# A graph layer with 1,327 row gathers: each gather from the table also waits for the landing of the gather three in front of it

## The chip, the cores and the metric

The kernel runs on one core of a Trainium2 chip. The time is device microseconds (us) of one execution of the program. The kernel before was timed three times: 2152.66, 2145.68 and 2149.95 us, a median of 2149.95 us. The profile comes from a further execution of its own, with a time of 2145.14 us, whose instructions span 2143.3 us.

The engines are named as in the profile: PE (matmul), PEld (PE's weight load), DVE (vector), ACT (scalar), POOL (GpSimd), SP (sync). Here POOL issues the gathers, SP and ACT issue the other DMAs.

## The reference: what is computed

```python
x, src, dst, edge                     # (12500, 64), (200000,), (200000,) sorted, (200000, 32)
msg_in     = concat([x[src], x[dst], edge])                 # 200000 x 160
messages   = relu(msg_in @ mW1 + mb1) @ mW2 + mb2           # hidden 128, out 64
aggregated = segment_sum(messages, dst, 12500)
update     = relu(concat([x, aggregated]) @ uW1 + ub1) @ uW2 + ub2
out        = layernorm(x + update)
```

The edges are sorted by their destination, so the destinations of neighbouring edges lie in a short window of nodes. The sources are random, so `x[src]` needs a real gather.

## The kernel before

The 200,000 edges are cut into 1,563 tiles of 128 edges, and six tiles make a step (`SUB = 6`), 261 steps in all. In a setup phase PE multiplies all nodes by the source part of `mW1` and by the destination part (`products`, L637), and the results go to tables in DRAM: `tab_a` by ACT's queue (L649), `tab_b` with the bias by SP's (L658). A row of a table is 128 floats, 512 bytes. From then on each step does this:

- **Gather** (`fetch`, L237). For a tile of the step, one indirect DMA issued by POOL fetches 128 rows of `tab_a`, those of the tile's 128 sources, into the step's buffer `xg`, 64 KB. In the first eight steps (`XG = 8`) the table is not ready yet, and 48 gathers fetch rows of `x` instead, which PE transposes and multiplies (L324, L427). In 118 steps (`COPIED`) two of the six tiles aren't gathered: ACT and DVE copy the nodes one column at a time from a transposed `x` that lies on chip (L379, L387), and PE multiplies them (L411). So 1,279 gathers read `tab_a`.
- **Edge part** (`edge_part`, L408). SP loads the edge features and the destinations into `l`, and windows of `tab_b` into `rhs`; DVE turns destinations into a selection (L271, L279). PE multiplies `l` by `rhs` into `pc`.
- **Node part** (`node_part`, L435). PE adds the gathered rows to `pc` by a matmul with the identity, four matmul records a step. This is the only reader of a gather from `tab_a`.
- **Sum** (`positive`, `collect`). DVE applies relu (L448), and one step later PE adds the result into the destinations' sums (L481) and counts (L477). Every few steps a block of nodes is finished (`update`, `residual`, `norm`, `store`).

The order is written out by hand in one loop over the steps. In the loop, `gather(s)` takes a buffer and lists the gathers of a step, `frees` says which earlier step must have been read for that, and `gathered <= s + XG` keeps gathers up to eight steps ahead of the step in which PE reads them; there are nine buffers (`ROWB = 9`). `fetch` issues one gather. Its argument `behind` names an instruction of PE (or, in the setup, of ACT) whose end the gather waits for, so that the gathers of a step are spread over it:

```python
for u in units[:1] if paced else units:
    fetch(u)
...
done = collect(s - 1)
n = (len(units) + 1) // 2
for k in range(n):
    fetch(units.pop(0), done[(k + 1) * len(done) // n - 1])
```

POOL's queue holds nothing but gathers from the setup to the end of the loop. Each gather reports its landing on one of eight semaphores in turn (`DMASW0` to `DMASW7`), and a gather waits until the one eight in front of it, the last user of its semaphore, has landed.

Of the kernel before, what the change touches and what calls it, by code (L numbers as in the profile page):

```python
# [37 lines left out]
XG = 8  # L38
# [34 lines left out]
U8 = mybir.dt.uint8  # L73
YBASE = XBASE + 4 * XCOLS
LEAD = 8
PACE = ((11, 0.48), (50, 0.505), (130, 0.483), (170, 0.469), (261, 0))
FINAL = 258


def progress(s):  # L80

    return sum(r * max(0, min(s + 1, b) - a) for (a, r), (b, _) in zip(PACE, PACE[1:]))

# [42 lines left out]
def gnn_kernel(ctx: ExitStack, tc: tile.TileContext, x1T, x, eT, e_rows, src, src_row, dst, dst_row, wlist, wrow, wnext, whalf,  # L126
# [77 lines left out]
    wb = const.tile([SUP, NSUP], I32, name="wb")  # L204

    rows = ctx.enter_context(tc.tile_pool(name="rows", bufs=ROWB))
    xg = {}

    def frees(s):

# [22 lines left out]
    def fetch(unit, behind=None):  # L233

        s, i = unit
        t, a = s * SUB + i, xg[s][1]
        ins = nc.gpsimd.indirect_dma_start(  # L237
            out=a[:, i, :] if s < XG else a[:, i // 2, i % 2, :], out_offset=None, in_=A[:, :] if s >= XG else x[:, :],
            in_offset=bass.IndirectOffsetOnAxis(ap=src_s[:, t:t + 1], axis=0))
        if behind is not None:  # L240
            tc.add_manual_dep(ins.ins, behind.ins.name,
                              mybir.DependencyInfo(mybir.DependencyClass.Sync, mybir.DependencyReason.DATA), reason="pace")

    with tc.tile_pool(name="work", bufs=2) as work, tc.manual_schedule():
# [83 lines left out]
        def columns_list():  # L328

            cols = work.tile([P, 2, 2, P], I32, name="cols", tag="tb", bufs=4)  # L330
            for r in range(2):
                n = min(P, NSUB - 1 - LEAD - r * P)
                v = src_row[:, ((LEAD + r * P) * SUB + SUB - 2) * P:]
                nc.sync.dma_start(cols[:n, r].rearrange("k b e -> k (b e)"),
# [6 lines left out]
        def portion(s, own):  # L341

            found = []
            for j, c in enumerate(COPIED):
                total = own(j)
                lo, hi = (min(max(int((progress(s + d) - j) * total / CHUNK + 1e-6) * CHUNK, 0), total) for d in (-1, 0))
                if lo < hi:
                    if c not in xc:
                        xc[c] = work.tile([P, P], F32, name="xc", bufs=3)
                    found.append((xc[c], c - LEAD, lo, hi, j))  # L350
            return found
# [347 lines left out]
        for u in first[:AHEAD]:  # L699
            fetch(u)  # L700
# [18 lines left out]
        for k, c in enumerate(range(0, NB, NCH)):  # L719
            copied = chunk_a(c)  # L720
            for i, u in enumerate(first[:EACH]):
                fetch(u, None if i else copied)
            first = first[EACH:]
            if k == 2:
                chunk_b(0, [B0v, Bv])
            if k == 3:
                nc.vector.tensor_tensor(drc[:, :8 * SUP], dst_s[:, :8 * SUP], early, op=ALU.subtract)
                first_nodes(0, 8)
            if k == 4:

                w0 = wint[:, :GE * SUP // SUB * LS]
                nc.vector.tensor_scalar(past, w0[:, GE * SUP // SUB * LS - 1:], float(EARLY - WIN), None, op0=ALU.is_gt)
                nc.vector.tensor_scalar(w0, w0, float(EARLY - WIN), None, op0=ALU.min)
                windows(0)
                windows(1)
            if k in (5, 7):
                g = (k - 5) // 2
                select_rows(g)
                load(g)
                select(g)  # L740
                counts(g)
            if k == 10:
                offsets()
# [97 lines left out]
        for s in range(last + 2):  # L841
# [6 lines left out]
            for u in units[:1] if paced else units:  # L848
                fetch(u)
# [267 lines left out]
```

## Time and profile before

| what | number |
|---|---|
| runs | 2152.66, 2145.68, 2149.95 us; median 2149.95 us |
| profiled execution: time, span | 2145.14 us, 2143.3 us |
| busy: PE, ACT, POOL, DVE | 1701.7, 1573.7, 1253.8, 1132.0 us |
| mean granted TensorE clock | 0.782 of full speed |
| DMA moved, mean rate | 190.59 MB, 89 GB/s |
| gathers from `tab_a`: number, issued from, to | 1,279, 80.3 us, 2091.3 us |
| the matmuls that read them: first, last start | 141.9 us, 2123.6 us |

In the lines of the profile, `L237 POOL DMA_INDIRECT xg<-tab_a,src_s x1279` is a group of instructions: source line, engine, operation, what is written and read, and how many. "busy" is the time for which such an instruction ran on its engine; for a gather that is the making of its descriptors, and the bytes move later. "idle before" is the engine's idle time ahead of the group with what ended it: "issue" means nothing that the profile shows, "remote" a semaphore whose writer the profile doesn't have. The chain is the work that ended last, followed back from the end of the program; a piece "DMA xg<-tab_a,src_s" in it runs from the issue of a gather to the semaphore of its landing. q0 is the queue of the gathers, q1 that of SP's DMAs, q10 that of ACT's.

### The profile page before, as it was taken

How to read it: one execution, taken by the hardware profiler on the slowest of the kernel's cores; microseconds unless marked ns; L12 is line 12 of the kernel's file. 1: busy time of each engine (PE TensorE's matmuls, PEld its weight loads, DVE VectorE, ACT ScalarE, POOL GpSimd, SP SyncE). 2: the span in 40 equal slices, each digit the busy share in tenths (PEclk: the TensorE clock that was granted, in tenths of full speed). 3: DMA queues.
4: the chain of work that ended last, by engine and by line, in shares of the span. 5: the costliest groups of instructions: out<-in, count | busy, mean ns of one | idle time of the engine just before them, and what ended most of it. 6: DMA issues, size and time to landing. Idle time of an engine off the chain costs nothing.

```text
span 2143.3 us, 50649 instructions
## 1 busy us (share of the span) xinstructions
PE 1701.7 (79%) x10742; PEld 1279.7 (60%) x10742; DVE 1132.0 (53%) x8036; ACT 1573.7 (73%) x8029; POOL 1253.8 (59%) x1336
## 2 busy tenths in 40 slices
PE   3487778797787788877888878887878888888788
PEld 3365556565565566656566656665665666666566
DVE  2215655565555555565555545455555565555553
ACT  1155887669869797798687877787867877787872
POOL 6565665666666656555655555565556656556660
PEclk7667887877787877777787877788778878887889
DMA  8452333332222223232233323233333333333331
GB/s 231 125 130 75 96 87 96 89 92 71 80 74 78 77 76 80 76 85 78 76 82 83 88 78 88 80 94 84 82 89 81 86 93 88 88 88 87 85 92 51
DMA packets 207847, 190.59 MB, mean 89 GB/s; under 512 B 57909, under 2 KB 174093, under 8 KB 207549
## 3 DMA queue, kind: packets, MB, share of 16 engines
q0 software_dynamic: 42464, 85.48, 16.1%
q1 hardware_dynamic: 150396, 92.86, 15.4%
q10 hardware_dynamic: 14690, 8.99, 1.5%
q8 instruction: 101, 1.65, 0.3%
q14 instruction: 196, 1.61, 0.2%
HBM read 169.15 MB, written 18.02 MB: 87 GB/s over the span
## 4 chain that ended last, share of the span: by engine, by line
PE 64%; issue 18%; DVE 9%; another core or an unknown queue 3%; DMA 2%; POOL 2%; DVEq 1%; ACT 0%; SPq 0%; ACTq 0%; POOLq 0%
PE sums L481 20%; PE pc L435 17%; PE pc L408 13%; DVE xc L387 4%; PE cnt L477 3%; DVE h L448 2%; PE cps L545 2%; PE cps L543 2%; POOL xg L237 2%; PE pc L411 2%; PE sums L529 2%; PE sums L530 1%; DVE l L271 1%; DMA xg<-tab_a,src_s 1%
## 5 line engine op out<-in xcount | busy, mean ns | idle before, releaser
L237 POOL DMA_INDIRECT xg<-tab_a,src_s x1279 | 1207.3, 944 | 812.5 <-issue 263.1
L379 ACT ACTIVATE xc<-xtop,xbot 128x1 f32 x7872 | 1490.7, 280 | 183.6 <-issue 161.6
L387 DVE TENSOR_TENSOR xc<-xtop,xbot 128x1 int32 x7232 | 607.2, 155 | 472.0 <-issue 457.8
L481 PE MATMUL sums<-band,h 128*128 128x96 f32 x3126 | 532.7, 324 | 134.8 <-issue 86.3
L481 PEld LDWEIGHTS sums<-band,h 128*128 128x128 f32 x3126 | 470.0, 230 | 170.0 <-issue 106.3
L435 PE MATMUL pc<-xg,band 128*128 128x384 f32 (+1 forms) x1008 | 465.4, 590 | 34.8 <-issue 30.7
L408 PE MATMUL pc<-rhs,l 64*128 64x128 f32 x3126 | 371.7, 354 | 77.2 <-issue 60.8
L408 PEld LDWEIGHTS pc<-rhs,l 64*128 64x128 f32 x3126 | 294.5, 238 | 123.9 <-issue 90.9
L448 DVE TENSOR_SCALAR h<-pc 128x768 f32<-128x768 f32 x252 | 240.3, 953 | 202.4 <-PE sums L481 83.7
L435 PEld LDWEIGHTS pc<-xg,band 128*128 128x128 f32 x1008 | 223.2, 244 | 154.8 <-issue 106.9
L271 DVE TENSOR_TENSOR l<-l,cps 128x768 f32<-128x768 int32 (+1 forms) x134 | 127.1, 949 | 146.1 <-PE pc L435 41.0
L477 PEld LDWEIGHTS <-one 128*1 128x1 bf16 x1563 | 59.5, 81 | 225.0 <-issue 218.9
L477 PE MATMUL cnt<-band,one 128*1 128x32 bf16 x1563 | 100.8, 180 | 54.6 <-issue 53.5
L552 ACT ACTIVATE y<-cps 128x256 f32<-128x256 f32 (+1 forms) x36 | 13.6, 379 | 157.5 <-issue 91.9
L411 PE MATMUL pc<-band,xc 64*128 64x128 f32 x472 | 80.4, 318 | 23.0 <-issue 19.3
L535 ACT ACTIVATE hTu<-sums,ub_s 128x416 f32<-128x416 f32 (+1 forms) x36 | 21.6, 599 | 100.9 <-remote 35.5
L279 DVE TENSOR_TENSOR band<-cps,drc 128x384 f32<-128x384 f32 x131 | 71.6, 546 | 25.4 <-PE pc L408 24.5
L637 PE MATMUL pb<-band,xtop 64*128 64x128 f32 x200 | 45.9, 395 | 42.8 <-DVE tb L645 21.9
L411 PEld LDWEIGHTS pc<-band,xc 64*128 64x128 f32 x472 | 64.2, 229 | 22.8 <-issue 22.5
L637 PEld LDWEIGHTS pb<-band,xtop 64*128 64x128 f32 x200 | 39.0, 283 | 47.6 <-DVE tb L645 23.0
L237 POOL DMA_INDIRECT xg<-in_x,src_s x48 | 45.5, 948 | 25.3 <-issue 13.5
L545 PE MATMUL cps<-u2c,hTu 128*128 128x64 f32 x284 | 54.4, 342 | 6.4 <-issue 6.0
(104 smaller groups left out, 630.5 us busy)
## 6 DMA issues: line engine op xcount, KB each, us to landing
l<-in_dst_row SPq DMA_DIRECT2D x262, 96.0 KB
l<-in_eT SPq DMA_DIRECT2D x262, 96.0 KB
xg<-tab_a,src_s POOLq DMA_INDIRECT x1279
rhs<-tab_b SPq DMA_DIRECT2D x361, 32.0 KB
tab_b<-tb SPq DMA_DIRECT2D x13, 512.0 KB
rhs<-tab_b SPq DMA_DIRECT2D x387, 16.0 KB
tab_a<-tb ACTq DMA_DIRECT2D x12, 512.0 KB
out<-y SPq DMA_DIRECT2D x35, 128.0 KB
```

The source lines that it names most:

```text
L237: ins = nc.gpsimd.indirect_dma_start(out=a[:, i, :] if s < XG else a[:, i // 2, i % 2, :], out_offset=None, in_=A[:, :] if s >= XG else x[ ...
L271: nc.vector.tensor_tensor(l[r], l[r].bitcast(I32), node[r].unsqueeze(2).broadcast_to([r.stop - r.start, SUP // 2, P]), op=ALU.is_equal)
L379: nc.scalar.activation(o[:, e:e + 1], top.bitcast(F32), AF.Identity, bias=bot.bitcast(F32))
L387: nc.vector.tensor_tensor(o[:, e:e + 1].bitcast(I32), top.bitcast(I32), bot.bitcast(I32), op=ALU.bitwise_or)
L408: done = nc.tensor.matmul(pc[:, b, k, :], L[g][q:q + 64, m, :], rhs[g % 2][q:q + 64, w, :], start=k == 0, stop=False)
L411: done = nc.tensor.matmul(pc[:, b, k, :], xc[s][q:q + 64], w1a[q:q + 64], start=False, stop=False)
L435: added = nc.tensor.matmul(pc[:, b, :m], ident, a[:, b, :m], start=False, stop=True)
L448: nc.vector.tensor_scalar(h, pc, 0.0, None, op0=ALU.max)
L477: nc.tensor.matmul(pn[:, bass.ds(ws[i], WIN)], one, SB[g][:, k0 + i, :, 1], start=False, stop=ends and i == n - 1)
L481: made.append(nc.tensor.matmul(ps[:, bass.ds(ws[i], WIDE * WIN)], h[:, i % 2, i // 2, :], widened(g, k0 + i), start=False, stop=ends and i ...
L545: nc.tensor.matmul(py[:, i], hT[:, i * P:(i + 1) * P], u2c, start=False, stop=i + 1 == blocks(u))
L637: nc.tensor.matmul(pb[:, h, i, :], (xbot if h else xtop)[64 * h:64 * h + 64, (c + HB * h + i) * P:(c + HB * h + i + 1) * P], w[64 * h:64 * ...
```

## The change

A list keeps every gather that was issued. A gather that reads `tab_a` gets a second dependency: besides the instruction `behind`, it waits for the semaphore of the gather three in front of it (`flight[-3:][:1]`). The gathers of the first eight steps get none.

```diff
+FLIGHT = 3
...
-    xg = {}
+    xg, flight = {}, []
...
         ins = nc.gpsimd.indirect_dma_start(
             out=a[:, i, :] if s < XG else a[:, i // 2, i % 2, :], out_offset=None, in_=A[:, :] if s >= XG else x[:, :],
             in_offset=bass.IndirectOffsetOnAxis(ap=src_s[:, t:t + 1], axis=0))
-        if behind is not None:
-            tc.add_manual_dep(ins.ins, behind.ins.name,
+        waited = [] if s < XG or len(flight) < FLIGHT else flight[-FLIGHT:][:1]
+        flight.append(ins)
+        for other in waited + [behind] * (behind is not None):
+            tc.add_manual_dep(ins.ins, other.ins.name,
                               mybir.DependencyInfo(mybir.DependencyClass.Sync, mybir.DependencyReason.DATA), reason="pace")
```

No instruction changes its place on any engine, and no wait changes on PE, DVE, ACT or SP. Only the waits of POOL's gathers differ. The first gathers from `tab_a` on POOL, before; `DMAHW` are semaphores of the setup's stores to the table, `DMASW` those of gathers:

```order
L237 DMA xg_452<-tab_a_63,src_s_68 128x128 [waits DMAHW4_49,DMAHW3_49,DMAHW5_49,DMAHW2_49,DMAHW7_49,DMAHW0_49,DMASW0_49]
L237 DMA xg_452<-tab_a_63,src_s_68 128x128 [waits DMASW1_49]
L237 DMA xg_452<-tab_a_63,src_s_68 128x128 [waits DMASW2_49]
L237 DMA xg_452<-tab_a_63,src_s_68 128x128 [waits DMASW3_49]
L237 DMA xg_452<-tab_a_63,src_s_68 128x128 [waits DMASW4_49]
```

The same five gathers after:

```order
L238 DMA xg_452<-tab_a_63,src_s_68 128x128 [waits DMAHW3_49,DMAHW4_49,DMAHW2_49,DMAHW5_49,DMAHW0_49,DMAHW7_49,DMASW5_49,DMASW0_49]
L238 DMA xg_452<-tab_a_63,src_s_68 128x128 [waits DMASW6_49,DMASW1_49]
L238 DMA xg_452<-tab_a_63,src_s_68 128x128 [waits DMASW7_49,DMASW2_49]
L238 DMA xg_452<-tab_a_63,src_s_68 128x128 [waits DMASW3_49,DMASW0_49]
L238 DMA xg_452<-tab_a_63,src_s_68 128x128 [waits DMASW4_49,DMASW1_49]
```

These five wait for one semaphore more each, until the wait for the third in front implies that for the eighth.

In the loop, on POOL at a place some thirty steps in, before; `PE` is the pacing instruction:

```order
L237 DMA xg_7324<-tab_a_63,src_s_68 128x128 [waits DMASW4_49]
L237 DMA xg_7324<-tab_a_63,src_s_68 128x128 [waits DMASW5_49,PE_49]
L237 DMA xg_7324<-tab_a_63,src_s_68 128x128 [waits DMASW6_49,PE_49]
L237 DMA xg_7324<-tab_a_63,src_s_68 128x128 [waits DMASW7_49,PE_49]
L237 DMA xg_7699<-tab_a_63,src_s_68 128x128 [waits DMASW0_49]
```

The same gathers after:

```order
L238 DMA xg_7324<-tab_a_63,src_s_68 128x128 [waits DMASW1_49]
L238 DMA xg_7324<-tab_a_63,src_s_68 128x128 [waits DMASW2_49,PE_49]
L238 DMA xg_7324<-tab_a_63,src_s_68 128x128 [waits DMASW3_49,PE_49]
L238 DMA xg_7324<-tab_a_63,src_s_68 128x128 [waits DMASW4_49,PE_49]
L238 DMA xg_7699<-tab_a_63,src_s_68 128x128 [waits DMASW5_49]
```

Each gather has as many waits as before. The wait for the semaphore of the eighth in front (its own number) has turned into one for that of the third in front, five numbers further.

## The prediction

> **What bounds the kernel now.** I read the page first: how busy the engines are, what the chain that ended last consists of, and what the gathers look like in the groups.
>
> ```profile
> span 2143.3 us, 50649 instructions
> PE 1701.7 (79%) x10742; PEld 1279.7 (60%) x10742; DVE 1132.0 (53%) x8036; ACT 1573.7 (73%) x8029; POOL 1253.8 (59%) x1336
> ...
> PE 64%; issue 18%; DVE 9%; another core or an unknown queue 3%; DMA 2%; POOL 2%; DVEq 1%; ACT 0%; SPq 0%; ACTq 0%; POOLq 0%
> ...
> L237 POOL DMA_INDIRECT xg<-tab_a,src_s x1279 | 1207.3, 944 | 812.5 <-issue 263.1
> ```
>
> PE is the bound: 79% busy and 64% of the chain, while POOL is 59% busy and 2% of the chain. POOL has 812.5 us of idle time in front of its gathers, so it can be held up by much in sum before it runs short. The question is where a single wait would fall, and whether PE would notice.
>
> For that I read the lines of the gather and of the matmul that reads it (the view by source line), for their first and last starts.
>
> ```profile
> L237 POOL DMA_INDIRECT xg<-tab_a,src_s x1279: 938/944/1475, 80.3 to 2091.3; - x183
> L237 POOLq EVENT_SEMAPHORE  x1034: 17/17/43, 12.4 to 2087.0; - x173
> ...
> who waited for it (us, times):
>   PEld pc L435: 5.1, 9
>   PE pc L408: 4.5, 4
> ```
> ```profile
> L435 PE MATMUL pc<-xg,band x1008: 376/486/1009, 141.9 to 2123.6; 128*128 128x384 f32 x87, 128*128 128x256 f32 x81
> ```
>
> The first gather is issued at 80.3 and its reader starts at 141.9: 61.6 us ahead. At the end it is 2091.3 against 2123.6, still 32.3 us. In between the code holds eight steps of lead, and a step lasts (2123.6 − 141.9) / 252 = 7.9 us (1,008 reading matmuls, four a step), so a step's gathers are begun some 60 us before they are read. The few microseconds that "who waited for it" puts on gathers (the largest 5.1 us in 9 times) can hardly be that: the matmul waits on several semaphores, each shared by every eighth gather, and a gather for a later step that lands in that moment moves the same semaphore. I take them as put down wrongly, and price the other reading among the rivals.
>
> Next, how close together gathers come, on POOL's timeline at the place where DMA is fullest:
>
> ```profile
> 102.07 0.94 POOL L237 DMA_INDIRECT xg<-tab_a,src_s  x1 [0.30 <-issue]
> 103.32 0.94 POOL L237 DMA_INDIRECT xg<-tab_a,src_s  x1 [0.30 <-issue]
> 104.57 0.94 POOL L237 DMA_INDIRECT xg<-tab_a,src_s  x1 [0.30 <-issue]
> 105.82 0.95 POOL L237 DMA_INDIRECT xg<-tab_a,src_s  x1 [0.30 <-issue]
> 108.69 0.94 POOL L237 DMA_INDIRECT xg<-tab_a,src_s  x1 [1.93 <-PE pc L408]
> 109.94 0.94 POOL L237 DMA_INDIRECT xg<-tab_a,src_s  x1 [0.30 <-issue]
> ```
>
> Even unhindered, a gather starts 1.25 us after the last one (0.94 of work and 0.30 of pause). So the third in front was started at least 105.82 − 102.07 = 3.75 us earlier. **The new wait costs nothing where a gather lands, and POOL takes note, within 3.75 us.** How long a landing takes stands in the chain, in nine pieces spread over the program; here are the first, the shortest, the two longest and the last:
>
> ```profile
> 400.26 2.31 DMA xg<-tab_a,src_s
> 652.90 3.35 DMA xg<-tab_a,src_s
> ...
> 1255.47 2.23 DMA xg<-tab_a,src_s
> ...
> 1726.21 3.48 DMA xg<-tab_a,src_s
> ...
> 2028.39 2.29 DMA xg<-tab_a,src_s
> ```
>
> They run from 2.23 to 3.48 us, mostly near 2.3. What POOL needs after a semaphore wait is passed stands in the chain between 393 and 394 us: 0.02 for the wait, then 0.21 to the start of the gather.
>
> ```profile
> 393.46 0.02 POOLq L237
> 393.47 0.21 issue
> 393.68 0.94 POOL xg L237
> ```
>
> **The change part by part.**
>
> *The wait in the loop.* 2.31 + 0.23 = 2.54 us against 3.75: 1.2 us to spare. The longest, 3.48 + 0.23 = 3.71, still fits by 0.04. In flight before the change are therefore, at the moment a gather is issued, two others as a rule; the new limit is already kept. Cost 0 for nearly all of the 1,279. A gather that lands later than 3.5 us would delay the next but two by the excess, a few tenths. What is queued behind the waiting gather is only more gathers, since nothing else is in POOL's queue there; and who waits for those is PE's L435, tens of microseconds later. The cover is that lead, 32 us at its shortest. If it were gone, every tenth would count once, on the step that reads the gather.
>
> *The wait in crowded stretches.* The setup's transfers and the first steps' large loads overlap the first gathers. By stretches:
>
> ```profile
> 80.00:100.00 20.00, 11.38 (x105) 9.24 (x104) 2.78 (x4) 2.53 (x5) 13.20 (x14) 0.83 0.53 137
> 100.00:112.00 12.00, 7.69 (x67) 6.45 (x68) 1.26 (x3) 4.58 (x6) 7.94 (x9) 0.80 0.78 188
> 120.00:130.00 10.00, 8.04 (x48) 6.71 (x48) 0.95 (x1) 4.67 (x5) 6.49 (x7) 0.67 0.84 187
> 140.00:150.00 10.00, 9.20 (x53) 5.80 (x51) 1.82 (x2) 7.69 (x6) 6.27 (x8) 0.77 0.70 157
> 1200.00:1600.00 400.00, 326.18 (x2005) 241.61 (x2004) 217.59 (x1598) 309.84 (x1608) 236.04 (x251) 0.79 0.31 84
> ```
>
> The last but one number is the DMA engines' busy share: 0.53 to 0.84 in four stretches up to 150 us, 0.31 in the middle of the program. In the second of them, DMA by queue from 99.5 us to 108.4, and to 108.6:
>
> ```profile
> q1 hardware_dynamic: 1015, 1.34, 65.9%
> q0 software_dynamic: 95, 0.20, 13.2%
> ...
> xg<-tab_a,src_s POOLq DMA_INDIRECT x6
> ```
> ```profile
> q0 software_dynamic: 96, 0.20, 12.9%
> ```
>
> Over the program q0 moved 42,464 packets for 1,327 gathers, 32 each:
>
> ```profile
> q0 software_dynamic: 42464, 85.48, 16.1%
> ```
>
> Six gathers were issued from 99.5 on, and by 108.4 only 95 packets had moved: the third of them, that of 102.07, was one packet short of its end and finished by 108.6, some 6.4 us after its issue. The gather of 105.82 would now wait for it and start near 108.5 + 0.23 = 108.7, 2.9 us late. The one of 108.69 then can't start before 108.7 + 1.25 = 110.0, 1.3 us late, and the lateness goes at the next pause that PE sets (such as the 1.93 us in front of 108.69). So four stretches with about 3 us of lateness at most in each, on a dozen gathers whose readers start at 141.9 us and after, with up to 61.6 us of lead: cost 0.
>
> *The bounds of that.* From above: if each of the four delays reached PE in full, 4 × 2.9 = 11.6 us. From below: a gather that is held back leaves the DMA engines to SP's loads, and something does wait for these:
>
> ```profile
> DVE drc L592 <- DMA col_a<-in_wrow: 14.4, 2, 10.7
> ```
>
> A gather's part of the DMA engines there is 13.2% of 8.9 us for 95 packets, so 0.4 us for 32. Up to two gathers are held back in each stretch: 4 × 2 × 0.4 = 3.2 us of gain at most, if all of it lay on the chain. I take 0, nearest to the rows of the lead and of the loads (13.2% against 65.9% of the DMA, so the loads are late by themselves), and keep −3.2 and +11.6.
>
> *Added instructions.* The first five gathers from the table wait for one semaphore more each, at 17 ns a wait: 0.09 us, in POOL's idle time. Cost 0. PE, DVE, ACT and SP have the same instructions and waits.
>
> *A rule weighed.* The longest of all 1,279 gather issues took 1.475 us, the median 0.944; even the longest would add 0.53 us to the landing, 2.84 + 0.23 = 3.07 of 3.75. The Trainium skill, in "SBUF — State Buffer", section "A bandwidth-pool intuition that's wrong", says that a DMA issued from GpSimd which takes some 620 ns alone takes some 3,100 ns beside a vector copy in a two-port mode, because GpSimd can't write descriptors meanwhile. By that, an estimate from the page: a landing of 2.31 + 2.48 = 4.8 us, a gather each (4.8 + 0.23) / 3 = 1.68 us, 2,145 us in all instead of 2,011, and a time of some 2,280 us. This trace shows no such gather before the change.
>
> *The sum.* 2145.14 us for the profiled execution, plus 0. That execution lies 4.8 us below the median of the three runs, so the forecast for the median is 2149.9 us. Runs of this kernel lie within 0.3% of each other (2145.68 to 2152.66), and a change below 0.3%, 6.4 us, can't be told from none.
>
> **The rivals.**
>
> 1. *Slower: the late gathers reach PE.* Place: the steps after 141.9 us. For it speak the 5.1 us in 9 times in which PE is said to have waited for gathers; against it the 61.6 us of lead there. It decides from the point where lateness is handed from stretch to stretch until it exceeds the lead, or where the lead of a single gather is below 3 us. Price 11.6 us: 2161.5 us.
> 2. *Slower: landings are longer for POOL than the pieces show,* so that the limit of three sets the rate. POOL has (2091.3 − 80.3) / 1279 = 1.57 us for a gather, so three in flight suffice up to a landing of 3 × 1.57 − 0.23 = 4.5 us. Against it: the longest of nine pieces is 3.48. If all landed as in the crowded stretch, after 6.4 us, a gather would take (6.4 + 0.23) / 3 = 2.21 us and all of them 2,827 instead of 2,011: some 2,960 us; with landings of 4.6 us it would be some 40 us. The rule of the Trainium skill's page "SBUF — State Buffer" that was weighed above is one way into this rival.
> 3. *Faster: fewer gathers among the loads.* Speaking for it: DVE's 14.4 us behind one of the loads. Price 3.2 us at most, 2146.7, which is inside what can't be told; for 6.4 us sixteen gathers would have to move out of the way of loads that the chain waits for.
> 4. *The limit never binds at all,* not even in the crowded stretches, because spacing by PE is wider than there. Then the time is the same 2149.9, and only the trace could tell.
>
> **How the numbers follow.** The forecast and rival 4, no change within 0.3%: 81%. Rival 1: 6%; rival 2, mostly in a weak form: 3%; slower for a reason that I don't see, 3%: 12% slower. Rival 3 or an unseen gain beyond 0.3%: 7%. The range takes the runs' own spread (−4.3, +2.7) and the two bounds: 2149.9 − 4.3 − 3.2 = 2142 below, and 2149.9 + 11.6 = 2162 above.
>
> **What would show it.** In the profile of the changed kernel: gathers still 1.25 us apart within a step from 200 us on, POOL's idle sum near 812 us, and the first and last reader at 142 and some 20 us before the end as now. Between 80 and 155 us a gather of four or so per stretch should start up to 3 us later, with a landing of a gather named as what ended POOL's wait. Wrong would be: POOL waiting for DMA all through the program, PE's L435 waiting for gathers by more than a few microseconds in sum, or SP's loads before 150 us ending clearly earlier.

## The result and the profile after

The changed kernel takes 2170.2 us (median, 2164.64 to 2173.93), the kernel before beside it 2148.07 us: a ratio of 1.0093, 95% interval 1.0073 to 1.0113. It is slower by some 20 us (22 by the medians, 20 by the ratio). The forecast was no change, with a range up to 2162.

The lines of the page that answer to those shown of before, then those of the gather and of its reader by source line (the change moves L237 to L238 and L435 to L438), and POOL's waits by what ended them:

```profile
span 2172.1 us, 50654 instructions
PE 1698.7 (78%) x10742; PEld 1282.5 (59%) x10742; DVE 1132.1 (52%) x8036; ACT 1576.5 (73%) x8029; POOL 1253.6 (58%) x1336
...
L238 POOL DMA_INDIRECT xg<-tab_a,src_s x1279 | 1207.1, 944 | 839.0 <-issue 258.2
```
```profile
L238 POOL DMA_INDIRECT xg<-tab_a,src_s x1279: 938/944/1140, 87.5 to 2115.4; - x183
...
L438 PE MATMUL pc<-xg,band x1008: 376/486/1009, 130.0 to 2149.2; 128*128 128x384 f32 x87, 128*128 128x256 f32 x81
```
```profile
POOL xg L238 <- DMA xg<-tab_a,src_s: 57.9, 75, 4.9
```

No engine does more work, and the new wait holds POOL for 57.9 us in 75 places, 4.9 us at the longest. The first reader starts at 130.0 us, 11.9 us *earlier* than before; the last one 25.6 us later. So it is not a delay that adds up from the start. Where the time goes is read from the readers: for each step, the start of its first L438 in the trace, minus the start in the trace of before.

```
step         8      9     10     11     12     13     14     20     32     64    128    192    256
after    -11.9  -11.7  -18.3  -18.8  -10.6   17.7   14.9   21.6   16.2   18.0   20.3   21.8   25.6
```

Up to step 11 the kernel is ahead by up to 18.8 us. Between the readers of steps 11 and 13 it loses 36 us, and after that next to nothing: 8 us over 243 steps. The same stretch in windows, after and then before (the columns are the window, its length, busy time of PE, PEld, DVE, ACT and POOL with their instructions, the granted clock, the DMA engines' share, GB/s):

```profile
100.00:120.00 20.00, 17.76 (x191) 15.49 (x190) 4.54 (x7) 13.01 (x13) 9.41 (x10) 0.93 0.68 166
120.00:140.00 20.00, 17.53 (x116) 13.26 (x116) 3.00 (x4) 17.06 (x13) 7.96 (x10) 0.66 0.80 178
140.00:160.00 20.00, 13.74 (x81) 8.33 (x82) 6.83 (x34) 0.00 (x0) 13.75 (x15) 0.85 0.29 77
160.00:200.00 40.00, 10.95 (x38) 6.92 (x39) 3.08 (x15) 0.00 (x0) 25.80 (x28) 0.50 0.20 51
```
```profile
100.00:120.00 20.00, 13.73 (x109) 11.59 (x109) 2.44 (x5) 7.99 (x10) 12.85 (x14) 0.68 0.59 144
120.00:140.00 20.00, 16.55 (x104) 14.13 (x106) 1.51 (x2) 9.59 (x9) 12.99 (x14) 0.67 0.59 133
140.00:160.00 20.00, 16.37 (x83) 11.35 (x82) 3.61 (x6) 12.87 (x9) 12.63 (x15) 0.67 0.55 132
160.00:200.00 40.00, 25.71 (x155) 17.82 (x153) 19.03 (x99) 16.46 (x89) 23.44 (x25) 0.71 0.30 80
```

From 100 to 140 us POOL issues 20 gathers instead of 28, and PE runs 307 matmuls instead of 213. From 160 to 200 us PE runs 38 instead of 155, while DMA is at 0.20. The early gain shows in PE's waits from 80 to 145 us; these are all that end by issue, first before, then after:

```profile
PE pc L427 <- issue: 13.6, 5, 7.8
PE pc L408 <- issue: 4.0, 7, 1.3
```
```profile
PE pc L411 <- issue: 2.2, 3, 1.1
PE cnt L480 <- issue: 0.5, 1, 0.5
```

What POOL does there and what PE does there stand on their timelines in the kernel after:

```profile
111.78 0.94 POOL L238 DMA_INDIRECT xg<-tab_a,src_s  x1 [4.30 <-DMA xg<-tab_a,src_s]
...
126.05 0.94 POOL L238 DMA_INDIRECT xg<-tab_a,src_s  x1 [4.45 <-DMA xg<-tab_a,src_s]
...
148.94 0.94 POOL L238 DMA_INDIRECT xg<-tab_a,src_s  x1 [0.31 <-issue]
150.18 0.94 POOL L238 DMA_INDIRECT xg<-tab_a,src_s  x1 [0.30 <-issue]
...
189.63 0.95 POOL L238 DMA_INDIRECT xg<-tab_a,src_s  x1 [0.30 <-issue]
190.88 0.95 POOL L238 DMA_INDIRECT xg<-tab_a,src_s  x1 [0.30 <-issue]
```
```profile
168.85 0.19 PE L480 MATMUL cnt<-band,one 128*1 128x32 bf16 x1 [0.62 <-issue]
172.33 0.19 PE L480 MATMUL cnt<-band,one 128*1 128x32 bf16 x1 [3.29 <-issue]
...
188.43 0.32 PE L484 MATMUL sums<-band,h 128*128 128x96 f32 x1 [2.48 <-issue]
191.24 0.32 PE L484 MATMUL sums<-band,h 128*128 128x96 f32 x1 [2.48 <-issue]
```

The held gathers (4.30 and 4.45 us) build up a backlog, and from 148 to 191 us POOL works it off: 35 gathers, 1.25 us apart but for one step of 2.0. Within this row single matmuls of 0.2 to 1.0 us stand 1.4 to 3.5 us apart, and what ended the pauses is "issue": no data and no semaphore that the profile shows. ACT runs nothing from 140 to 200 us, but for another reason: it waits 62.3 us for a transfer that SP issues late, behind a wait of its own. In the trace of before the same pauses of PE are there in small: the share of PE's time that is idle by issue, from one microsecond after the start of the n-th gather of an unbroken row on (210 to 2080 us), is about 5% for n = 1, then 9, 23, 38, and over 40% for n = 5 and 6; in the kernel after it is 6, 9, 24, 35, 45 and 48%. That is a coincidence in time, no proof of a cause; for that the runs below.

### The profile page after: what moved, and what is told of

The parts are those of the page before. It is cut to its first block, busy times and chain, and to the rows that moved or that the text cites. A ratio compares the mean times of both kernels' runs of the same rounds, so it can differ in the third digit from the quotient of the medians.

```text
span 2172.1 us, 50654 instructions
## 1 busy us (share of the span) xinstructions
PE 1698.7 (78%) x10742; PEld 1282.5 (59%) x10742; DVE 1132.1 (52%) x8036; ACT 1576.5 (73%) x8029; POOL 1253.6 (58%) x1336
## 3 DMA queue, kind: packets, MB, share of 16 engines
q1 hardware_dynamic: 150396, 92.86, 15.3%
## 5 line engine op out<-in xcount | busy, mean ns | idle before, releaser
L238 POOL DMA_INDIRECT xg<-tab_a,src_s x1279 | 1207.1, 944 | 839.0 <-issue 258.2
L484 PE MATMUL sums<-band,h 128*128 128x96 f32 x3126 | 538.5, 325 | 153.5 <-issue 106.7
L484 PEld LDWEIGHTS sums<-band,h 128*128 128x128 f32 x3126 | 475.1, 231 | 188.9 <-issue 121.9
L438 PE MATMUL pc<-xg,band 128*128 128x384 f32 (+1 forms) x1008 | 452.0, 575 | 29.6 <-issue 27.0
L411 PE MATMUL pc<-rhs,l 64*128 64x128 f32 x3126 | 364.4, 351 | 80.7 <-issue 55.4
L411 PEld LDWEIGHTS pc<-rhs,l 64*128 64x128 f32 x3126 | 288.0, 234 | 128.0 <-issue 81.2
L438 PEld LDWEIGHTS pc<-xg,band 128*128 128x128 f32 x1008 | 216.6, 237 | 145.9 <-issue 94.0
L414 PE MATMUL pc<-band,xc 64*128 64x128 f32 x472 | 77.3, 314 | 14.2 <-issue 14.1
L546 PE MATMUL cps<-ux,xw 128*128 128x64 f32 x284 | 54.2, 342 | 6.5 <-issue 6.3
```

The source lines that it names most:

```text
L238: ins = nc.gpsimd.indirect_dma_start(out=a[:, i, :] if s < XG else a[:, i // 2, i % 2, :], out_offset=None, in_=A[:, :] if s >= XG else x[ ...
L411: done = nc.tensor.matmul(pc[:, b, k, :], L[g][q:q + 64, m, :], rhs[g % 2][q:q + 64, w, :], start=k == 0, stop=False)
L414: done = nc.tensor.matmul(pc[:, b, k, :], xc[s][q:q + 64], w1a[q:q + 64], start=False, stop=False)
L438: added = nc.tensor.matmul(pc[:, b, :m], ident, a[:, b, :m], start=False, stop=True)
L484: made.append(nc.tensor.matmul(ps[:, bass.ds(ws[i], WIDE * WIN)], h[:, i % 2, i // 2, :], widened(g, k0 + i), start=False, stop=ends and i ...
```

## The experiments

**Theory A:** the limit makes a backlog where DMA is full, and the unbroken row in which POOL catches up starves PE, which then pauses by "issue". **Theory B:** the wait costs at each gather, all through the program. **Theory C:** the crawl near 150 to 200 us has to do with the setup's transfers, not with the row.

### Where: the limit late alone, early alone

```diff
-        waited = [] if s < XG or len(flight) < FLIGHT else flight[-FLIGHT:][:1]
+        waited = [] if s < 26 or len(flight) < FLIGHT else flight[-FLIGHT:][:1]
```

> The limit of three in flight only for gathers of step 26 and later, which are issued after some 190 us. Theory A (the loss is the backlog that the limit builds up in the crowded stretches before 150 us, and the unbroken row of gathers that works it off, during which PE's instructions come at a crawl): within 0.3% of before. Theory B (the wait costs something at every gather; POOL has 57.9 us of waits for landings in the changed kernel's trace): 0.5 to 0.9% slower. Theory C (as A, but PE's crawl comes from the crowded DMA of the setup, not from the row of gathers): within 0.3%.

Measured: 2151.13 us against 2149.11, 1.0024 (1.0004 to 1.0044), although POOL waits for landings as often as in the kernel after; no single wait is longer than 1.8 us:

```profile
POOL xg L238 <- DMA xg<-tab_a,src_s: 41.0, 78, 1.8
```

```diff
+        waited = [] if not XG <= s < 26 or len(flight) < FLIGHT else flight[-FLIGHT:][:1]
```

> The limit only for gathers of steps 8 to 25. Theory A: 0.7 to 1.2% slower than before, the whole loss, with an unbroken row of some 30 gathers between 145 and 195 us and PE below half its usual busy share in it. Theory B: within 0.3%. Theory C: 0.7 to 1.2% slower.

Measured: 2162.49 us, 1.0060 (1.0041 to 1.0079). Its steps 8 to 11 are 13.7 to 20.9 us ahead of before, step 12 is 16.2 us behind, and 17.8 us stay to the end; a row of 29 gathers stands from 141 to 176 us, and PE is busy for 7.98 of 36 us there. By the median it is just below the 0.7 to 1.2% that A expected. Eighteen steps of 253 carry most of the loss, which is against B; the other 235 steps cost at most 0.44%. The two parts make 15.4 us of the 22, the rest lies within the intervals. A and C are not told apart by this.

### A row in the quiet middle: gathers held back in the program

The kernel before, without the limit; the gathers of 6 (and of 3) steps from step 120 on are left for later.

```diff
+            if 120 <= s < 120 + 6:
+                held, units = held + units, []
+            elif s == 120 + 6:
+                units = held + units
```

> No limit; the kernel before, but in the quiet middle (step 120 on) the gathers of six steps are held back and issued in one go at step 126, some 33 in a row, which still leaves two steps, 16 us, until the first of them is read. Theory A: PE crawls during the row as in the changed kernel (there 27 us were lost beside 35 gathers), so 18 to 30 us lost, 0.8 to 1.4% slower. Theory B and C: the lead covers it, within 0.3%.

> As e3, but the gathers of three steps are held back and issued at step 123, some 18 in a row. Theory A: a part of e3's loss, 6 to 14 us, 0.3 to 0.7% slower. Theory B and C: within 0.3%.

Measured: 1.0034 (1.0020 to 1.0047) for 6 steps, 1.0041 (1.0026 to 1.0055) for 3. A step's shift goes from −3.1 to +4.1 us across the place in the first, from +2.8 to +8.5 in the second. The design was weak: held gathers lose the PE instruction that paces them, so POOL issued them as soon as buffers were free, in rows of 8 to 11 rather than 33. In the row of 11 of the first, 1030 to 1044 us, PE is busy for 5.91 of 14 us (42%, against 79% in the 30 us ahead of it). The direction fits A. For 6 steps the size is below what A said; for 3 it is within it, but that kernel's setup was some 7 us late by itself, as long as the step in question.

### A row of gathers that nobody reads, the same POOL time without gathers, the same bytes without POOL

Each is the kernel before with one insertion at step 126, near 1096 us in the runs. The targets are columns of `drc` that are read no more.

```diff
+            if s == 126:
+                for k in range(24):
+                    nc.gpsimd.indirect_dma_start(out=drc[:, k % 4 * DH:(k % 4 + 1) * DH], out_offset=None, in_=A[:, :],
+                        in_offset=bass.IndirectOffsetOnAxis(ap=src_s[:, k:k + 1], axis=0))
```

> The kernel before, with 24 gathers more in the quiet middle, at step 126 (about 1012 us), each of 128 rows of tab_a, into a spare 128 x 128 place, with no wait that binds. POOL is busy with them for about 24 x 1.25 = 30 us and then with the 17 or so gathers that became due meanwhile: a row of about 40 gathers, 1.25 us apart. Their data are used by nothing, and the real ones have 61 us of lead. A (a row without a break starves PE's issue): 12 to 30 us slower, 1.006 to 1.014, with PE idle by issue for 40% or more of the row and steps stretched there only. B (the wait at each gather costs): no wait here, within 0.3%. C (crowded setup DMA makes PE crawl): none here, within 0.3%.

Measured: 2215.89 us against 2183.59, 1.0136 (1.0117 to 1.0155), all at the insertion: shift 18.2 us at step 120, 50.1 at step 128. (The trace of before was taken when that kernel took some 34 us less, so a part of each shift is not the insertion's: this run and the next two are 6.5 to 7.7 us behind at step 56 already.) Windows of 36 us ahead of the row, in it and behind it:

```profile
1060.00:1096.00 36.00, 26.69 (x161) 20.19 (x161) 22.14 (x167) 28.06 (x150) 20.55 (x23) 0.71 0.33 91
1096.00:1132.00 36.00, 8.12 (x35) 5.88 (x35) 6.37 (x44) 12.51 (x54) 27.23 (x29) 0.59 0.22 60
1132.00:1168.00 36.00, 23.28 (x147) 18.04 (x149) 11.47 (x86) 14.53 (x75) 18.09 (x20) 0.74 0.22 60
```

In the row of 29, PE is busy for 8.12 of 36 us, DVE and ACT fall with it, and DMA is less busy than ahead of it. The costliest waits of the three in that window all end by issue:

```profile
DVE sums_s L506 <- issue: 22.1, 1, 22.1
PE sums L481 <- issue: 21.2, 9, 3.2
...
ACT xc L379 <- issue: 18.9, 24, 1.2
```

Nothing waits for these data, and no setup is near: C is out. The loss, 32 us, is just above what A expected (12 to 30).

```diff
+            if s == 126:
+                for k in range(50):
+                    nc.gpsimd.memset(drc[:, :4 * DH], float(k))
```

> The kernel before, with 50 memsets of 128 x 512 on POOL at the same place, about 26 us in all: POOL is busy as long as in the run with 24 gathers, but no DMA comes of it; then the 16 or so gathers that became due run in a row. A, if it is the gathers that starve PE: during the memsets PE runs with less issue idle than before (under 18%), up to 5 us gained; in the row of 16 after them 5 to 9 us lost; in sum -2 to +8 us, under 0.4%. Rival D (any work on POOL starves PE, or POOL's share of a port): PE crawls during the memsets too, 12 us or more slower.

Measured: 2204.46 us, 1.0087 (1.0070 to 1.0103): far more than the 0.4% that A allowed in sum. The windows show where: the memsets, then the row of 37 real gathers after them.

```profile
1063.00:1099.00 36.00, 29.54 (x177) 21.42 (x176) 22.17 (x172) 34.29 (x183) 22.18 (x27) 0.74 0.30 82
1099.00:1124.00 25.00, 23.84 (x212) 18.97 (x207) 17.20 (x135) 23.07 (x122) 22.53 (x44) 1.00 0.17 49
1124.00:1170.00 46.00, 12.50 (x61) 9.93 (x56) 10.71 (x66) 15.21 (x67) 34.67 (x38) 0.56 0.25 66
```

While POOL is full of memsets, PE is busy for 95% (82% ahead of them) and the steps gain 2 us. In the catch-up row it is busy for 27%, and the steps lose 28 us (12.0 at step 128, 39.8 at 136). By the waits, 14.2 us of PE's idle time there are issue, and 15.3 are one wait for a semaphore whose writer the profile doesn't have; DVE's column copies stand idle by issue for 33.2 of the 46 us, ACT's for 29.2. I had taken a row of 16 for the overdue gathers alone; it lasts until the gathers that fall due meanwhile are done too, 37. So POOL's work as such (rival D) is not it; the gathers in a row are.

```diff
+            if s == 126:
+                for k in range(24):
+                    nc.sync.dma_start(drc[:, k % 3 * DH:(k % 3 + 1) * DH], A[P * k:P * k + P, :])
```

> The kernel before, with 24 plain transfers of 128 rows of 512 bytes from tab_a into three spare places, issued by SP at the same place, each after the landing of the third in front: the same bytes as 24 gathers in some 25 to 60 us, with POOL left as it was. A, if POOL's own descriptor work is the cause: within 0.3%, and PE's issue idle there as before. Rival E (the traffic of 64 KB transfers itself starves PE): 5 to 15 us slower, with PE's issue idle over 30% there.

Measured: 2184.70 us, 1.0005 (0.9989 to 1.0021). SP issued the 24 transfers within 17.5 us, one per 0.73 us, each behind the landing of the third in front: denser than the gathers, which follow at 1.25 us. The lines are SP's issues, the window around them, and the two costliest waits of PE in it:

```profile
1093.20 17.51 SPq L850 DMA_DIRECT2D drc<-tab_a  x24
```
```profile
1093.00:1115.00 22.00, 10.91 (x61) 7.30 (x63) 10.20 (x78) 18.75 (x99) 11.36 (x12) 0.78 0.43 117
```
```profile
PE pc L408 <- DMA rhs<-tab_b: 9.0, 1, 9.0
PE pc L408 <- issue: 1.3, 3, 0.5
```

PE waits once, 9.0 us, for a load that SP issued behind the 24, and its issue idle is 2.1 of 22 us, where E expected over 30%. So the same number of bytes, moved faster but by SP's queue, does not do what the row of gathers does: E is out for traffic of this kind.

### Breaking the row

The kernel after, with a stricter wait for each fourth gather of the steps 8 to 59.

```diff
+        if XG <= s < 60 and len(flight) % 4 == 0:
+            waited = flight[-1:]
```

> The kernel after, in which at steps 8 to 59 each fourth gather waits for the landing of the gather right in front instead of the third: so no row there is longer than four. A: the row of 35 is gone, PE's busy share from 160 to 200 us goes from 27% (after) back to 55% or more, and 15 to 30 us of the loss come back: 2140 to 2158 us. B (each wait costs what it holds POOL for): the waits are longer, so it is as slow as after or slower: 2170 us or more. C: PE crawls in 160 to 200 us as in after, within 5 us of after's time.

Measured: 2252.20 us, 1.0307 (1.0289 to 1.0325), the opposite of what A expected of the total. The steps show two parts. Up to step 20 it is 16 to 27 us ahead of before, and no row of six stands between 72 and 568 us. But four gathers take more than the 4 × 1.57 us at which they are needed (1.78 us a gather from 150 to 565 us), so the lead is used up: PE waits 106.1 us for gathers (35 times) between 150 and 565 us, and step 56 is 25.2 us behind (some 7 of them as in the three runs above). At step 60 the rule ends, and the backlog comes as one row of 38:

```profile
530.00:568.00 38.00, 24.73 (x145) 18.44 (x146) 17.63 (x144) 27.86 (x150) 19.79 (x21) 0.69 0.24 64
568.00:616.00 48.00, 14.67 (x69) 9.88 (x68) 5.59 (x42) 4.84 (x27) 35.42 (x38) 0.57 0.23 60
```

PE is busy for 31% of it, and step 64 is 69.8 us behind: 45 us for one row. The row moved to where the waits ended, and its cost with it. This is what A says of a row, and it refutes my remedy.

### Spacing the gathers

Which property of the row does it: that the gathers have no break (A1), or that each takes a fixed piece of PE's supply (A2)? Memsets on POOL ahead of gathers make breaks. First, one of 128 x 512 ahead of each of the 24; it writes columns 512 to 1023 of `drc`, and so changes node numbers that later tiles compare with.

```diff
                 for k in range(24):
+                    nc.gpsimd.memset(drc[:, 4 * DH:8 * DH], 0.0)
```

> The run with 24 gathers more, in which a memset of 128 x 512 on POOL (525 ns in the run with 50 of them) stands ahead of each of the 24, so that they follow each other at 1.8 us instead of 1.25. A1 (it is the density of the row that starves PE; 26 us of PE's work were lost in a row of 29 gathers): the row does not starve PE; 3 to 12 us slower than before, the rest being the real gathers that come late and run in a row after it. A2 (each gather takes a fixed piece of PE's supply, about 1 us each): as slow as the run without memsets, 1.011 to 1.016.

Measured: 1.0157 (1.0128 to 1.0187), but not an answer: DVE's select of a later tile reads those columns and waited for POOL.

```profile
DVE band L279 <- POOL drc L850: 29.9, 1, 29.9
```

Before that wait reached PE, though, eight gathers stood 1.66 us apart, and PE was busy for 13.32 of 13.5 us:

```profile
1083.00:1096.50 13.50, 13.32 (x94) 9.11 (x92) 6.95 (x53) 13.50 (x73) 11.96 (x17) 0.91 0.30 82
```

Then memsets of 128 x 64 ahead of every gather from the table, one or three in the kernel before, two in the kernel after:

```diff
+        for k in range(1 if s >= XG else 0):
+            nc.gpsimd.memset(spare, float(k))
         ins = nc.gpsimd.indirect_dma_start(
```

> The kernel before with one memset of 128 x 64 on POOL (about 0.15 us) ahead of each gather from tab_a, 1279 of them, so that gathers in a row stand 1.4 us apart instead of 1.25; POOL has 812 us of idle time to cover 192 us of memsets. A1: PE's issue idle falls below the 291 us of before, 5 to 60 us faster. A2: within 0.3%. Against both, if POOL's time were short: slower by 0.3% or more, with rows longer than before.

> As the run with one memset, but three (about 0.45 us): gathers at 1.7 us, which is above the 1.57 us at which they are needed on the average, in the places where they stand in a row. A1: PE's issue idle in rows falls further than with one memset, but a backlog can build up; -80 to +20 us. A2: within 0.3%, or slower where the gathers come late.

> The kernel after with two memsets of 128 x 64 (about 0.3 us) ahead of each gather from tab_a: the catch-up row of 35 from 148 to 191 us is run at 1.55 us apart instead of 1.25. A1: the row starves PE less; the loss against before, 22 us in the kernel after, falls to 5 us or less, or turns into a gain. A2: as slow as after, 1.007 to 1.012, since there are as many gathers in as much of PE's time.

Measured: 1.0027 (1.0011 to 1.0043), 1.2526 (1.2491 to 1.2561) and 1.1340 (1.1309 to 1.1372). One memset changed little, and the 5 to 60 us that A1 expected to gain did not come: a pause of 0.30 us became 0.17 of memset and 0.16 of pause, so gathers stood 1.28 us apart, and PE's issue idle is 312 us (296 in before). With two and three they stood mostly 1.87 and 2.08 us apart, and POOL became the bound: 1279 × 2.08 = 2,660 us of the 2693.08. PE's issue idle is 159 and 174 us there, the direction of A1, but PE waits 467 and 605 us for DMAs, behind which issue time can hide, so this decides little. The last two show the early gain again: their steps 8 to 17 were 20 to 36 us ahead of before while gathers were sparse.

The next four were to settle A1 against A2, with two memsets of 128 x 192 into columns that are read no more, or one of 256 bytes a partition ahead of every gather (of before, and of after), or two of 128 x 64 in steps 8 to 19 alone.

```diff
                 for k in range(24):
+                    for _ in range(2):
+                        nc.gpsimd.memset(drc[:, 4 * DH:4 * DH + 192], 0.0)
```
```diff
+        if XG <= s < NSUB:
+            nc.gpsimd.memset(spare.bitcast(U8), 0)
```
```diff
+        for k in range(2 if XG <= s < 20 else 0):
+            nc.gpsimd.memset(spare, float(k))
```

> The run with 24 gathers more, with two memsets of 128 x 192 (0.26 us each by the durations of 64 and 512 columns) ahead of each of the 24, into columns that nobody reads any more: they follow each other at 1.65 to 1.9 us, for 40 to 46 us, and some 28 real ones then run in a row. A1: in the spaced row PE is busy for 60% or more of the time (79% over the span of before, 20% in the unbroken row), and the loss, 15 to 30 us, comes in the row of real ones after it. A2: PE is busy for under 45% in the spaced row too, and the loss is 45 us or more.

> The kernel before with one memset of 128 x 256 bytes on POOL ahead of each gather from tab_a: gathers in a row 1.3 to 1.45 us apart instead of 1.25. A1: PE's issue idle falls as the distance grows; at 1.4 us or more 5 to 40 us faster, at 1.3 us within 0.3%, as with 64 columns. A2: within 0.3% at any distance.

> The kernel after with the same memset: the catch-up row at 1.3 to 1.45 us. A1: at 1.4 us or more the loss against before falls from 0.9% to 0.5% or less; at 1.3 us it stays at 0.7 to 1.2%. A2: 0.7 to 1.2% at any distance.

> The kernel before with two memsets of 128 x 64 ahead of each gather of steps 8 to 19 alone: 72 gathers at up to 1.87 us, so that the early steps are 20 to 30 us ahead of before, as in the runs with memsets at all gathers. A: the backlog (72 x 0.3 to 0.6 us, some 20 to 45 us of gathers) is then run without a break, and the gain is given back: 2140 to 2170 us. Rival G (the early gain is of its own and stays): 2115 to 2135 us.

Beside these four the kernel before took 1687.66 us, 21 to 23% less than the 2149.11 to 2183.59 us of all runs above. Measured against that: 1729.43 us, 1.0244 (1.0227 to 1.0261); 1943.76, 1.1517 (1.1497 to 1.1536); 1987.70, 1.1768 (1.1744 to 1.1792); 1725.37, 1.0228 (1.0211 to 1.0245). The profile of the first shows how (the kernel before has no trace of its own from that time); POOL from 58 to 861 us, far from the insertion, where the code is that of before, the engines from 100 to 860 us, and PE's largest idle time by issue, there and in the trace of before:

```profile
L237 POOL DMA_INDIRECT xg<-tab_a,src_s x638 | 603.3, 946 | 194.4 <-issue 124.6 <-DMA xg<-tab_a,src_s 18.9 <-PE pc L435 18.3
```
```profile
100.00:860.00 760.00, 608.82 (x4676) 473.76 (x4680) 510.84 (x3834) 731.10 (x3852) 574.72 (x609) 0.88 0.40 105
```
```profile
PE pc L435 <- issue: 26.0, 19, 4.9
```
```profile
PE sums L481 <- issue: 86.3, 124, 2.1
```

Some 640 gathers stand in one unbroken row, 1.25 us apart, and nobody is starved: ACT is busy for 96%, and PE has 28 us of issue time in the whole span, where the trace of before has 296 (the sums of all its lines of this kind; the 291 of the expectations is some 2% low). POOL's rate is the bound there (1,327 × 1.25 = 1,659 us), and the insertion costs just what it takes of POOL: 22.9 us of gathers, 12.8 of memsets and 7.5 of pauses are 43.2 us, measured 41.8. The 72 spaced gathers of steps 8 to 19 cost 37.7 us in the same way, so on the early gain (rival G) that run says nothing. The limit costs there too, in a plainer way: the kernel after with memsets takes 43.9 us more than the kernel before with them, and its POOL waits as much:

```profile
POOL xg L241 <- DMA xg<-tab_a,src_s: 43.8, 109, 4.5
```

Two of the four were run again, for the case that the kernel before would take about 2150 us.

> The run with 24 gathers more and two memsets of 128 x 192 ahead of each, a second time. Where the kernel before takes about 2150 us: A1: in the spaced row (24 gathers at about 1.75 us) PE is busy for 60% or more of the time, and the loss, 15 to 30 us, comes in the row of real gathers after it. A2: PE is busy for under 45% in the spaced row too, and the loss is 45 us or more. Where it takes about 1690 us: 40 to 43 us slower, as at the first time, by POOL's own time (24 x 1.75 = 42 us).

> The kernel before with one memset of 128 x 256 bytes (0.33 us) ahead of each gather, a second time: gathers at 1.46 us in a row. POOL's own bound is 1327 x 1.46 = 1940 us, the time of the first time. Where the kernel before takes about 2150 us: A1: PE's issue idle falls well below 291 us, and the kernel becomes 20 to 200 us faster. A2: within 0.5%. If a row at 1.46 us starves PE as one at 1.25 us does, and lasts longer: 1% or more slower.

The kernel before took 1687.99 us, and the ratios were 1.0240 (1.0219 to 1.0262) and 1.1513 (1.1488 to 1.1538), as at the first time. A1 against A2 stays open; the clearest piece on it is the 13.5 us above, which speaks for A1. No version beat the kernel before, neither beside its 2150 to 2184 us nor beside its 1688.

## Why the prediction was wrong

- **The step that failed** is "The wait in crowded stretches", and in it the sentence "four stretches with about 3 us of lateness at most in each … with up to 61.6 us of lead: cost 0". Two things in it were wrong. The lateness was handed on: POOL waited 18.8 us for landings in 9 places from 80 to 150 us, up to 4.9 us at once, instead of ending at the next pause. (Another 7.2 us of the backlog are the later first gather, 87.5 against 80.3; a run without the limit, the one that holds 3 steps, had such a setup too, so this need not come from the change.) And the lead covers only data. What PE lost was not a late gather: it paused by issue while POOL caught up, and no term of the sum stood for that. The row cost 36 us here, and 28, 32 and 45 us in three runs that made such a row elsewhere.
- **The bounds of that step** had a price for each delay that reaches PE, 11.6 us, and for DMA relief, −3.2 us. Up to step 11 the change was worth −18.8 us, six times the lower one: with gathers held back, PE was busy for 17.76 instead of 13.73 of 20 us. PE's idle time by issue from 80 to 145 us falls from 17.6 to 2.7 us, the largest change among its waits there, and PE itself waits for no load in either. So the gain is of the same kind as the later loss, with fewer gathers instead of a row of them. The run with 50 memsets, in which PE is busy for 95% while no gather runs, fits that; for the first steps themselves no run tried it.
- **"The wait in the loop", cost 0,** held nearly: with the limit from step 26 on, 2.0 us by the medians (1.0024, 1.0004 to 1.0044). POOL waits 41.0 us there, in 78 places, more than the few tenths that I expected of a late landing; the lead covers nearly all of it, with no wait over 1.8 us and no row of more than eight gathers behind 72 us.
- **Rival 1** has the side and about half of the size (2161.5), but not the mechanism: it needed readers that wait for gathers, and the loss is issue. Its side came out by luck. **Rival 2**, landings that set the rate, did not happen in these runs: from 200 us on the gathers keep pace. **Rival 3** has the side of what happened up to step 11, by idle time of another kind than it named, and that gain was then paid back twice over. **Rival 4** is refuted by 75 waits.
- **The line I passed over** was quoted at the start of the prediction: "issue 18%" of the chain. I read PE's 64% as the bound and did not ask when the 18% occur. Counted by the position of a gather in its row, the trace of before pointed at the answer.
- **Of the signs I had named,** the late gathers between 80 and 155 us with a landing named came as said, and the last reader starts 22.9 us before the end, some 20 as forecast. POOL's idle sum is 839.0 instead of near 812, and the first reader starts at 130.0 instead of 142: it fits gathers that press on PE even without waits, which no step of the prediction had.
- **The rule weighed** changed nothing: no gather's issue took over 1.140 us in the kernel after, so the lengthening that the Trainium skill's page "SBUF — State Buffer" (section "A bandwidth-pool intuition that's wrong") describes for a DMA from GpSimd beside a DVE copy isn't seen here. PE, on the other side, was slowed.

## What to carry to other kernels

A wait in front of queued transfers does not only delay them, it bunches them: ask what the catch-up does to the engines beside it, not only whether the data still arrive in time. Slack that covers the data is no cover for that. And where a chain of waits holds a large share of time that nothing shown explains, find what else runs at those moments before pricing any change in the rhythm of that.

## What was not expected of the hardware

- Where the kernel before took about 2150 to 2184 us, PE starved beside each of the five long rows of gathers that POOL issued 1.25 us apart: it was busy for 22 to 31% in rows of 29 to 38, against 65 to 89% in the stretch ahead of them, with DMA at 0.20 to 0.25. ACT and DVE stood idle by issue too in two rows in the middle of the program (18.9 and 24.5 us of 36, 29.2 and 33.2 of 46); near the setup they waited for others. POOL busy with memsets for 29 us did not do it (95%), nor did 24 transfers of 64 KB that SP issued 0.73 us apart.
- Beside the last six runs the kernel before took 1688 us, rows of over 600 gathers starved nobody, and PE's granted clock over a run of that kernel was 0.88 to 0.89 instead of 0.77 to 0.80. What sets the two times apart the runs do not show. Chip number 0 stands with a set at 2150.55 us and with one at 1687.99, so that number alone doesn't decide it; and the difference is there ahead of any gather from the table, the first of which is issued at about 64 us instead of 80 to 88.
- By which path a row of gathers slows PE where it does, the runs do not show either. The Trainium skill, "Runtime: NRT & Kernel Launch", section "Instruction fetch mechanics", says that an engine's sequencer fetches the next block of instructions while the current one runs, and that what crossing into a new block costs is mostly hidden. That fits the 28 us of issue time beside the 1688 us and not the 296 us beside the 2150, where matmuls that wait for nothing shown stand up to 3.5 us apart. What the traces have of fetching doesn't explain these: in the row of 29 gathers two packets of 8 KB moved on the queues of kind "instruction" within 36 us, while PE paused ahead of every matmul from 1102 us on, and the packets of 16 KB took 1.07 us in the trace of before and 1.08 in that of the first run beside 1688 us (medians, 200 to 1600 us). Whether an engine was handed its instructions late is not in the traces.
